# A four-layer image network on one core: layer statistics by ScalarE, buffers lent after layer 1, and the last image's bases by products

## Chip, cores and metric

The program runs on one core of a Trainium2 chip. The metric is the device time of one execution in microseconds (us); for several executions it is the median. The engines are named as in the profile: PE is TensorE (matmuls), DVE is VectorE, ACT is ScalarE, POOL is GpSimd, SP is SyncE, whose queue issues the DMA transfers here.

## What is computed

The input x has 8 images of 32 channels and 256 x 256 places, in fp32. Four layers are applied, each as x + f(group_norm(x)) with 16 groups of two channels:

```
layer 0: 1x1 convolution; its output is also pooled to 5x5 a channel, and that 5x5 is
         the channel's own filter: a 5x5 depthwise convolution of the output
layer 1: q = round(clip(v / 2^-7, -127, 127));  out[o] = -sum over c, 3x3 of |q - w[o]| * 2^-7
layer 2: 3x3 convolution with bias
layer 3: on 8x8 windows, y = layernorm over channels; four functions "kan":
         kan(v) = Ws . exp(-((layernorm(v) - grid_k) / (4/7))^2)  (8 grid points k)
                + Wb . silu(v) + b
         kan1 and kan2 on two 16-wide rearrangements of y, kan3 on y, kan4 on their sum z
```

The group norms need the mean and the variance of whole images, so each layer of an image must be complete before its norm is known.

## The kernel before

**Tiling.** A tile has 128 partitions: 4 row bands of the image times 32 channels. F = 2048 words is 8 rows of 256 places in each band; an image is 8 such chunks (NCH). Between layers the images lie in DRAM (x1, q, x2, x3).

**Stages.** `stage0` is layer 0 in two passes: the first loads 8 chunks, takes statistics (`add_stats`, four `bn_stats` of 512 columns a chunk, L643) and row sums for the pooling (`pool`, L749); the second loads chunks with a halo, does 25 taps of 16 small matmuls on PE (L892), evicts with ACT (L925), takes the statistics of the result, stores it, and at last quantises it (ACT L967, DVE `clip` L972 and L973). `stage1` is layer 1: the 16 passes of an image (4 row parts x 4 output groups) each make 72 distance tiles max(q - w, 0) of 128 x 4128 bf16, by DVE in one instruction (L996) or by ACT in two halves (L998), and PE adds each up with a selection matrix into the accumulator psA (L1018); when a pass is complete ACT evicts psA (L1065, called the gate), statistics are taken of the result, and it is stored. `stage2` is layer 2: load with halo, normalise on DVE (`normal`, L1131), 9 taps on PE (L1148), evict with ACT (L1164), statistics. `stage3` is layer 3, in 8 units an image: centring matmul, eviction (L1234), square (L1239), variance matmul into psV (L1247), 1/sqrt by Ln and Exp (`roots`, L1260 and L1264), broadcast by PE (L1279) and product on DVE (L1287). `kan` then makes 8 bases, each a Square (L1384) and an Exp (L1397) on ACT, and PE sums them into psB (L612), evicted by L1462. Silu runs on ACT (L1328, L1487) with another activation table than Exp and Ln, so each change of table is a load (L1562).

**Order of the work.** Nothing runs in the order in which it is written. Each piece becomes a task with an engine, a cost in us, a rank, its inputs and its buffers; `Plan.run` simulates the four queues while the program is built, always starting the ready task of the lowest rank whose buffers fit, and the instructions are then emitted in that order. Layer 1's distances are no tasks: `fill` makes them where DVE has nothing else ready, on ACT only for the first image or after 8 us without other ACT work (`slack`). PE gives layer 1's sums precedence when two or more distance tiles wait. Layer 1 of image b runs beside layer 3 of image b - 1 and layer 0 of image b + 1 or later. Tasks that need the Exp/Ln table or the Silu table are put into stretches in the order of writing, and a task of a later stretch waits until the earlier ones are all started. A task may have an alternative on another engine (`other`): the square of a basis can be done on DVE as a product (L1390); `run` allows it only when all passes of layer 1 are done.

**Buffers.** `ROOM` gives SBUF to one block of F/2 for psA's results (xr), three blocks for bases (bas), three for silus (si), and an arena of 10 F (sb) for everything else, bases in excess included when BASE_SPARE words stay free. Three distance tiles (dv) exist. In PSUM there are one psA, one psB and two psV. A kan's matmuls may open psB when its exp number HOLD is over.

Of the kernel before, what the change touches and what calls it, by code (L numbers as in the profile page):

```python
# [10 lines left out]
F32 = mybir.dt.float32  # L11
# [13 lines left out]
R = 8  # L25
# [5 lines left out]
DENOM = 4.0 / 7.0  # L31
EPS = 1e-5
# [35 lines left out]
ROOM = [("bas", 3 * BASE, BASE), ("si", 3 * F, F), ("rs", F // 2, F // 4), ("xr", F // 2, F // 2), ("sb", 10 * F, 0)]  # L68
AHEAD = 9.0
# [5 lines left out]
BASE_SPARE = 3 * F  # L75
HOLD = 4
# [14 lines left out]
class Buf:  # L91


    def __init__(self, kind, words=0):
        self.kind, self.words = kind, words
        self.writers, self.readers = [], []
        self.tile = None
        self.left, self.first, self.at, self.taken, self.base = 0, None, None, False, kind == "bas"
        self.spill = False
# [6 lines left out]
class Plan:  # L106
# [57 lines left out]
    def fits(self, need, spare):  # L164
# [3 lines left out]
        for b in need:  # L168
            if b.kind in ("dv", "bas") and b.spill:
                b.kind = "dv" if self.places["dv"] else "bas"  # L170
            if b.base:
                b.kind = "bas" if self.places["bas"] else "sb"
                spare = BASE_SPARE
            if b.kind in self.places and not self.places[b.kind]:
                return False
# [16 lines left out]
    def bases_full(self):  # L192
        return not self.places["bas"] and sum(n for _, n in self.free["sb"]) < F + BASE_SPARE
# [35 lines left out]
    def run(self):  # L229
# [23 lines left out]
        while left or any(not p.done for p in self.passes):  # L253
            moved = True
            while moved:
                moved = False
                for e in engines:
# [3 lines left out]
                    if best is None:  # L261
                        for t in ready[e]:
# [4 lines left out]
                            if t.eng != e and not all(p.done for p in self.passes[self.first_pass :]):  # L267
                                continue
# [4 lines left out]
                        if best is not None and e == "PE" and best.rank > self.image() + AHEAD:  # L273
                            piece = self.fill(e, False)
                            if piece is not None:
                                best = piece
                        if best is not None and best.n is not None:
                            ready[best.eng].remove(best)
                            if best.other:
                                ready[best.other[0]].remove(best)  # L280
                                if best.eng != e:
                                    self.sets[best.stretch][1] -= 1
# [71 lines left out]
    def image(self):  # L354
        return next((p.b for p in self.passes[self.first_pass :] if not p.done), len(self.passes))
# [92 lines left out]
def kernel(  # L448
# [49 lines left out]
    nc.vector.scalar_tensor_tensor(kbsq, kb, -1.0, kb, ALU.mult, ALU.mult)  # L498
    for n in range(5):
# [91 lines left out]
    def sb(b, n=None):  # L591
        return b.tile[:, : n or b.words] if b.tile is not None else arena[:, b.at : b.at + (n or b.words)]
# [25 lines left out]
    class Norm:  # L618
# [17 lines left out]

        def add_stats(self, src, at, r, rank, n=4):
# [8 lines left out]

        def finish(self):
# [5 lines left out]
            def first():  # L653
                for i in range(n):
# [3 lines left out]
            plan.add("DVE", 1.1 if n == 1 else 1.5, first, r=self.bufs, w=[small], rank=self.rank)  # L658
# [70 lines left out]
    def stage0(b, rank, span, after):  # L729
# [9 lines left out]
        for k in range(NCH):  # L739
            xt = Buf("sb", F)  # L740
            plan.add(
                "SP", 2.0, lambda k=k, xt=xt: by_block(lambda p, q: nc.sync.dma_start(sb(xt)[p], xn[k, q])),
# [3 lines left out]
            def pool(k=k, xt=xt):  # L746
                v = sb(xt).rearrange("p (r w) -> p r w", w=W)
# [3 lines left out]
            norm.add_stats(xt, 4 * k, [], r(0.02 * k))  # L751
            plan.add("DVE", 2.9, pool, r=[xt], w=[rs_buf[k]], rank=r(0.02 * k))
# [103 lines left out]
        for k in range(NCH):  # L856
# [60 lines left out]
            for n, t in enumerate(tap_order):  # L917
# [7 lines left out]
                lambda xt=xt: nc.scalar.activation(  # L925
                    sb(xt, F), psB.rearrange("p s f -> p (s f)"), AF.Identity, bias=bi
# [3 lines left out]
            norm1.add_stats(xt, 4 * k, [], rk)  # L930
# [23 lines left out]
        for h in range(NH):  # L954
            for j in range(0, NJ, 2):
# [15 lines left out]
                def clip(t=t):  # L971
                    nc.vector.tensor_scalar(sb(t, F), sb(t, F), QMAX, -QMAX, ALU.min, ALU.max)  # L972
                    nc.vector.tensor_scalar(q16(t), sb(t, F), ROUND, ROUND, ALU.add, ALU.subtract)  # L973

                plan.add("DVE", 2.5, clip, w=[t], rank=rk)
# [51 lines left out]
    def stage1(b, x1buf, qbuf):  # L1027
# [3 lines left out]
        for h in range(NH):  # L1031
# [16 lines left out]
            for g in range(NG):  # L1048
# [3 lines left out]
                ps.xr = xr = Buf("xr", F // 2)  # L1052
# [4 lines left out]
                            sb(xr)[p],  # L1057
# [7 lines left out]
                    lambda g=g, xr=xr: nc.scalar.activation(  # L1065
# [616 lines left out]
```

## Time and profile before

| what | value |
|---|---|
| median of 3 runs | 15807.77 us (15794.59 to 15817.06) |
| profiled execution | 15810.7 us, its span 15808.7 us |
| PE busy | 12814.9 us, 81% |
| DVE busy | 13427.1 us, 85% |
| ACT busy | 12262.5 us, 78% |
| granted PE clock, mean | 0.921 |
| distances on DVE (L996) | 8321 whole, 818 halves |
| distances on ACT (L998) | 972 halves |
| table loads (L1562) | 161 |

The span runs from the first to the last instruction of the profiled execution. Busy is the time in which an engine has an instruction under way. A line such as L996 is a line of the kernel before; a group's row gives its count, its busy time, the mean of one in ns, and the idle time of the engine ahead of it with what ended that. For most of the span three engines are busy at once, so the page's shares are means over stretches in which different engines are the tightest.

### The profile page before, as it was taken

How to read it: one execution, taken by the hardware profiler on the slowest of the kernel's cores; microseconds unless marked ns; L12 is line 12 of the kernel's file. 1: busy time of each engine (PE TensorE's matmuls, PEld its weight loads, DVE VectorE, ACT ScalarE, POOL GpSimd, SP SyncE). 2: the span in 40 equal slices, each digit the busy share in tenths (PEclk: the TensorE clock that was granted, in tenths of full speed). 3: DMA queues.
4: the chain of work that ended last, by engine and by line, in shares of the span. 5: the costliest groups of instructions: out<-in, count | busy, mean ns of one | idle time of the engine just before them, and what ended most of it. 6: DMA issues, size and time to landing. Idle time of an engine off the chain costs nothing.

```text
span 15808.7 us, 560681 instructions
## 1 busy us (share of the span) xinstructions
PE 12814.9 (81%) x260296; PEld 4330.4 (27%) x260296; DVE 13427.1 (85%) x12536; ACT 12262.5 (78%) x6849; POOL 33.1 (0%) x25
## 2 busy tenths in 40 slices
PE   6889897887897888888887888778878887887666
PEld 4223232322222222223222222222222222222222
DVE  2898989789878889888899999999999989997465
ACT  0888848678648778676778997799879987997687
POOL 0000000000000000000000000000000000000000
PEclk9989898998998999999999999999999999998777
DMA  4342345446435444554545554454544454444554
GB/s 117 74 101 55 99 118 160 108 123 169 98 97 157 130 118 125 140 139 105 133 123 142 140 131 126 114 140 123 130 127 130 127 128 129 130 132 112 148 154 134
DMA packets 1192870, 1970.85 MB, mean 125 GB/s; under 512 B 362752, under 2 KB 878848, under 8 KB 1092224
## 3 DMA queue, kind: packets, MB, share of 16 engines
q1 hardware_dynamic: 1190528, 1934.98, 46.6%
q8 instruction: 2036, 33.36, 0.9%
q14 instruction: 306, 2.51, 0.1%
HBM read 1162.83 MB, written 771.75 MB: 122 GB/s over the span
## 4 chain that ended last, share of the span: by engine, by line
PE 22%; ACT 20%; DVE 6%; issue 6%; DMA 1%; SPq 0%; DVEq 0%; ACTq 0%
PE psB L612 9%; PE psA L1018 7%; ACT bas L1384 5%; ACT bas L1397 4%; DVE dv L996 3%; ACT arena L1384 2%; PE psB L1148 2%; ACT arena L1397 2%; ACT arena L1234 2%; PE psB L892 1%; ACT si L1462 1%; ACT arena L1239 1%; DVE arena L1287 1%; PE psV L1247 1%; DVE arena L1390 1%
## 5 line engine op out<-in xcount | busy, mean ns | idle before, releaser
L996 DVE TENSOR_SCALAR dv<-qh,w1q 128x4128 bf16<-128x4128 bf16 (+1 forms) x8815 | 10491.2, 1248 | 1358.8 <-PE psA L1018 1289.9
L1018 PE MATMUL psA<-dv,sel_b 128*32 128x512 bf16 x71048 | 5420.4, 403 | 1421.8 <-DVE dv L996 1155.5
L1018 PEld LDWEIGHTS <-sel_b 128*32 128x32 bf16 x82944 | 2047.6, 97 | 6763.7 <-issue 5758.6
L1384 ACT ACTIVATE bas<-arena,kb 128x2048 f32<-128x2048 f32 x1396 | 2782.5, 1993 | 411.8 <-DVE arena L1287 258.6
L1397 ACT ACTIVATE bas<-bas 128x2048 f32<-128x2048 f32 x1396 | 2671.6, 1914 | 40.1
L998 ACT ACTIVATE dv<-qh,w1n 128x2064 bf16<-128x2064 bf16 x832 | 1635.9, 2009 | 1157.6 <-PE psA L1018 1042.0
L612 PE MATMUL psB<-bas,tl 32*32 32x512 f32 x48544 | 1953.2, 653 | 438.8 <-ACT bas L1397 240.1
L892 PE MATMUL psB<-arena,wt 32*32 32x512 f32 (+1 forms) x51040 | 1848.8, 606 | 122.2 <-issue 69.4
L612 PE MATMUL psB<-arena,tl 32*32 32x512 f32 x22368 | 918.8, 619 | 104.0 <-ACT arena L1397 29.0
L612 PEld LDWEIGHTS psB<-bas,tl 32*32 32x32 f32 x48544 | 526.5, 107 | 1327.5 <-ACT bas L1397 514.2
L892 PEld LDWEIGHTS psB<-arena,wt 32*32 32x32 f32 x51040 | 657.5, 104 | 814.0 <-issue 611.4
L1384 ACT ACTIVATE arena<-arena,kb 128x2048 f32<-128x2048 f32 x407 | 810.0, 1990 | 0.0
L1397 ACT ACTIVATE arena<-arena 128x2048 f32<-128x2048 f32 x407 | 779.1, 1914 | 11.6
L643 DVE BATCH_NORM_STATS2 tiny<-arena 128x6 f32<-128x512 f32 x768 | 473.7, 680 | 345.4 <-ACT arena L925 246.4
L1018 PE MATMUL psA<-qh,sel_b 128*32 128x512 bf16 x9216 | 666.3, 394 | 92.1 <-DMA qh<-q 76.8
L1287 DVE TENSOR_TENSOR arena<-psB,arena 128x2048 f32<-128x2048 f32 x280 | 640.0, 2286 | 59.0 <-PE psB L1279 55.9
L1462 ACT ACTIVATE si<-psB,cols_sb 128x2048 f32<-128x2048 f32 x192 | 377.0, 1963 | 385.0 <-PE psB L612 331.5
L612 PE MATMUL psB<-si,tl 32*32 32x512 f32 x14080 | 618.8, 624 | 32.4 <-DVE arena L1287 13.8
L1148 PE MATMUL psB<-arena,tl 32*32 32x510 f32 (+3 forms) x16384 | 626.6, 610 | 19.9 <-issue 19.8
L1239 ACT ACTIVATE arena<-arena 128x2048 f32<-128x2048 f32 x320 | 612.4, 1914 | 9.8
L925 ACT ACTIVATE arena<-psB,cc 128x2048 f32<-128x2048 f32 x64 | 125.6, 1962 | 536.0 <-PE psB L913 536.0
L1234 ACT ACTIVATE arena<-psB 128x2048 f32<-128x2048 f32 x224 | 418.9, 1870 | 127.1 <-PE psB L612 126.5
(151 smaller groups left out, 7406.4 us busy)
## 6 DMA issues: line engine op xcount, KB each, us to landing
arena<-x SPq DMA_DIRECT2D x128, 1024.0 KB
arena<-y SPq DMA_DIRECT2D x128, 1024.0 KB
si<-sy SPq DMA_DIRECT2D x512, 256.0 KB
arena<-in_x_dram SPq DMA_DIRECT2D x240, 384.0 KB
arena<-in_x_dram SPq DMA_DIRECT2D x256, 256.0 KB
x<-arena SPq DMA_DIRECT2D x256, 256.0 KB
xr<-x SPq DMA_DIRECT2D x512, 128.0 KB
x<-xr SPq DMA_DIRECT2D x512, 128.0 KB
```

The lines of the kernel that those rows point to most:

```text
L612: nc.tensor.matmul(view(o[j * C : (j + 1) * C, i - first, :]), w_, src(rows, i, j), start=start, stop=stop)
L892: nc.tensor.matmul(o[:, lo - 2 * j : hi - 2 * j, c0:c1], wt[rows, t, :], d[rows, lo + dy + 2 : hi + dy + 2, c0 + dx : c1 + dx], start=firs ...
L996: nc.vector.tensor_scalar(dst, src, w1q[:, at : at + 1], 0.0, ALU.subtract, ALU.max)
L998: nc.scalar.activation(dst, src, AF.Relu, bias=w1n[:, at : at + 1])
L1018: nc.tensor.matmul(psA[j * C : (j + 1) * C, i, :], sel_b[:, n, :], src[:, at : at + 2, t % 3 : t % 3 + W], **flags,)
L1148: nc.tensor.matmul(o[:, lo - 2 * j : hi - 2 * j, c0:c1], (wc if t == 4 else tl[:, W2T + t, :])[rows], d[rows, lo + dy + 1 : hi + dy + 1, c ...
L1234: lambda ps=ps, at=at: nc.scalar.activation(sb(c)[:, at], ps().rearrange("p s f -> p (s f)"), func, bias=shift),
L1239: plan.add("ACT", 1.9, lambda: nc.scalar.activation(sb(sq), sb(c), AF.Square), r=[c], w=[sq], rank=rk)
L1287: lambda ps=ps, at=at: nc.vector.tensor_tensor(sb(c)[:, at], ps().rearrange("p s f -> p (s f)"), sb(c)[:, at], ALU.mult),
L1384: lambda k=k, bas=bas: nc.scalar.activation(sb(bas), sb(rb), AF.Square, bias=kb[:, n, k : k + 1]),
L1397: lambda k=k, bas=bas, square=square: nc.scalar.activation(sb(bas), sb(bas), AF.Exp, scale=-1.0, bias=0.0 if square.eng == "ACT" else kbsq ...
L1462: nc.scalar.activation(sb(o), psB.rearrange("p s f -> p (s f)"), AF.Identity, bias=obias)
```

## The change

1. **Statistics.** `add_squares` takes the place of `add_stats`. The sum of a chunk comes out of the eviction that ACT does anyway, through its accumulator output (`accum_out`); for the first pass of layer 0 it comes from the pooling's row sums, less the columns that two bins share. A Square on ACT, shifted by the first chunk's mean, writes its squares as bf16 to spare room behind the chunk and gives their sum through the accumulator output. `first` makes mean and variance of these sums. The blocks grow for it: layer 0's first pass and layer 2 hold 1.5 F each, xr holds 3F/4.
2. **Layer 2's normalisation** moves from DVE to ACT.
3. **The clip** rounds first and clips then, in bf16.
4. **Lent buffers.** When all passes of layer 1 are done (`over`), the distance tiles may be bases or silus. In the same time evictions and squares of `variance` may run on DVE.
5. **The last image's bases.** Two of eight (k = 2 and 5) are made by Square and Exp. The others are products of a neighbour, a constant and one of two ratios, exp(2v) and exp(-2v) times a factor: one DVE instruction each, in the order of CHAIN. The bases' squares have no alternative on DVE there.
6. **The last image's silu** is v * exp(-ln(1 + exp(-v))): a clamp on DVE, three ACT instructions with the Exp/Ln table, a product on DVE.
7. HOLD goes from 4 to 3, BASE_SPARE from 3 F to 2 F, the test with AHEAD goes; the units' order is written anew (`beside`), with each piece given its rank.

The diff, cut:

```diff
+CHAIN = ((2, None), (5, None), (3, 2), (1, 2), (4, 5), (6, 5), (0, 1), (7, 6))
+MID, FAR, FAR2 = 3, 20.0, 50.0
...
-ROOM = [("bas", 3 * BASE, BASE), ("si", 3 * F, F), ("rs", F // 2, F // 4), ("xr", F // 2, F // 2), ("sb", 10 * F, 0)]
-AHEAD = 9.0
+ROOM = [("bas", 3 * BASE, BASE), ("si", 3 * F, F), ("rs", F // 2, F // 4), ("xr", 3 * F // 4, 3 * F // 4), ("sb", 10 * F, 0)]
...
-BASE_SPARE = 3 * F
-HOLD = 4
+BASE_SPARE = 2 * F
+HOLD = 3
...
             if b.base:
-                b.kind = "bas" if self.places["bas"] else "sb"
+                b.kind = "bas" if self.places["bas"] else "dv" if self.over() and self.places["dv"] else "sb"
                 spare = BASE_SPARE
+            if b.side:
+                b.kind = "si" if self.places["si"] or not self.over() else "dv" if self.places["dv"] else "sb"
...
-                        if best is not None and e == "PE" and best.rank > self.image() + AHEAD:
-                            piece = self.fill(e, False)
-                            if piece is not None:
-                                best = piece
...
+    def over(self):
+        return all(p.done for p in self.passes[self.first_pass :])
...
+        def add_squares(self, src, at, i, size, rank):
+            if not self.chunks & 1 << i:
+                self.chunks |= 1 << i
+                plan.add(
+                    "DVE", 0.16,
+                    lambda: nc.vector.tensor_scalar(
+                        self.shift[:, i : i + 1], self.sums[:, at : at + 1], -1.0 / size, None, ALU.mult
+                    ),
+                    r=[src, self.summed], w=[self.shifted[i]], rank=rank,
+                )
+            plan.add(
+                "ACT", 0.25 + 0.85e-3 * size,
+                lambda: nc.scalar.activation(
+                    sb(src)[:, size : size + size // 2].bitcast(BF16), sb(src, size), AF.Square, bias=self.shift[:, i : i + 1],
+                    accum_out=self.squares[:, at : at + 1],
+                ),
+                r=[src, self.shifted[i]], w=[self.bufs[at]], rank=rank,
+            )
...
             def first():
+                if self.chunks:
+                    mean, d, q = self.mv[:, :, 0], self.v, self.t
+                    for of, a in ((d, self.sums), (q, self.squares)):
+                        a = a[:, 0 : 2 * NH * n if n == 1 else NH * n].rearrange("p (n k) -> p n k", n=n)
+                        nc.vector.tensor_reduce(of, a, AX.X, ALU.add)
+                    count = float(HB * W // n)
+                    nc.vector.tensor_scalar(mean, d, 1.0 / count, None, ALU.mult)
+                    nc.vector.tensor_tensor(d, mean, self.shift, ALU.add)
+                    nc.vector.tensor_tensor(d, d, d, ALU.mult)
+                    nc.vector.scalar_tensor_tensor(self.mv[:, :, 1], q, 1.0 / count, d, ALU.mult, ALU.subtract)
+                    return
...
-            xt = Buf("sb", F)
+            xt = Buf("sb", 12 * W)
...
+                total, both = norm.sums[:, k : k + 1], norm.d[:, 0, 0:1]
+                nc.vector.tensor_reduce(total, rowsum[:, :, k * R : (k + 1) * R], AX.XY, ALU.add)
+                nc.vector.tensor_reduce(both, v[:, :, 51:205:51], AX.XY, ALU.add)
+                nc.vector.tensor_tensor(total, total, both, ALU.subtract)
...
-                    sb(xt, F), psB.rearrange("p s f -> p (s f)"), AF.Identity, bias=bi
+                    sb(xt, F), psB.rearrange("p s f -> p (s f)"), AF.Identity, bias=bi,
+                    accum_out=norm1.sums[:, k : k + 1],
...
-            norm1.add_stats(xt, 4 * k, [], rk)
+            norm1.add_squares(xt, k, 0, F, rk)
...
-                    nc.vector.tensor_scalar(sb(t, F), sb(t, F), QMAX, -QMAX, ALU.min, ALU.max)
                     nc.vector.tensor_scalar(q16(t), sb(t, F), ROUND, ROUND, ALU.add, ALU.subtract)
+                    nc.vector.tensor_scalar(q16(t), q16(t), QMAX, -QMAX, ALU.min, ALU.max)
...
-                norm.add_stats(xr, 8 * g + 2 * h, [], rk, 2)
+                norm.add_squares(xr, NH * g + h, g, F // 2, rk)
...
-                nc.vector.tensor_scalar(sb(xt), sb(xt), norm.mean, norm.rs, ALU.subtract, ALU.mult)
-            plan.add("DVE", 1.7, normal, r=[norm.done], w=[xt], rank=rk)
+                nc.scalar.activation(sb(xt, 10 * W), sb(xt, 10 * W), AF.Identity, bias=nmr, scale=norm.rs)
+            plan.add("ACT", 2.4, normal, r=[sm["c2"]], w=[xt], rank=rk)
...
+                evict.other = "DVE", 0.15 + 2.1 * us, lambda ps=ps, at=at: nc.vector.tensor_scalar(
+                    sb(c)[:, at], ps().rearrange("p s f -> p (s f)"), shift, None, ALU.add
+                )
+            square = plan.add("ACT", 1.9, lambda: nc.scalar.activation(sb(sq), sb(c), AF.Square), r=[c], w=[sq], rank=rk)
+            square.other = "DVE", 2.3, lambda: nc.vector.tensor_tensor(sb(sq), sb(c), sb(c), ALU.mult)
...
+        def silu(a, rk):
+            if not last:
+                plan.add("ACT", 1.9, lambda: nc.scalar.activation(sb(a), sb(a), AF.Silu), w=[a], rank=rk, table=SILU)
+                return
+            e = Buf("sb", F)
+            plan.add(
+                "DVE", 1.3, lambda: nc.vector.tensor_scalar(sb(e), sb(a), -FAR2, None, ALU.max),
+                r=[a], w=[e], rank=rk, spare=SPARE,
+            )
+            for func, scale_, bias in ((AF.Exp, -1.0, 0.0), (AF.Ln, 1.0, 1.0), (AF.Exp, -1.0, 0.0)):
+                plan.add(
+                    "ACT", 1.9,
+                    lambda func=func, scale_=scale_, bias=bias: nc.scalar.activation(
+                        sb(e), sb(e), func, scale=scale_, bias=bias
+                    ),
+                    w=[e], rank=rk, table=LN_EXP,
+                )
+            plan.add(
+                "DVE", 2.3, lambda: nc.vector.tensor_tensor(sb(a), sb(a), sb(e), ALU.mult), r=[e], w=[a], rank=rk
+            )
...
+            if last:
+                up, down = Buf("sb", F), Buf("sb", F)
+                plan.add(
+                    "DVE", 1.3,
+                    lambda: nc.vector.tensor_scalar(sb(up), sb(rb), kmax[:, n : n + 1], kmin[:, n : n + 1], ALU.min, ALU.max),
+                    r=[rb], w=[up], rank=rk, spare=SPARE,
+                )
+                for o, sign, bias in ((down, -2.0, kdn[:, n : n + 1]), (up, 2.0, kb2[:, n, MID : MID + 1])):
+                    plan.add(
+                        "ACT", 1.9,
+                        lambda o=o, sign=sign, bias=bias: nc.scalar.activation(
+                            sb(o), sb(up), AF.Exp, scale=sign, bias=bias
+                        ),
+                        r=[up], w=[o], rank=rk, table=LN_EXP, spare=SPARE,
+                    )
+            for k, k0 in chain:
+                bas = bases[k]
+                if k0 is not None:
+                    ratio = up if k > k0 else down
+                    by = float(np.exp(2 * (MID - k0) * (k - k0) - 1))
+                    exps.append(plan.add(
+                        "DVE", 2.4,
+                        lambda bas=bas, k0=k0, ratio=ratio, by=by: nc.vector.scalar_tensor_tensor(
+                            sb(bas), sb(bases[k0]), by, sb(ratio), ALU.mult, ALU.mult
+                        ),
+                        r=[bases[k0], ratio], w=[bas], rank=rk,
+                    ))
+                    continue
...
-                square.other = "DVE", 2.45, product
+                square.other = None if last else ("DVE", 2.45, product)
...
-                        "SP", 2.0 if name == "oa" else 8.0, load2, r=[db], w=[a], rank=rk, after=exps[4:5], spare=F,
+                        "SP", 2.0 if name == "oa" else 8.0, load2, r=[db], w=[a], rank=rk, after=exps[(0 if last else 4) :][:1], spare=F,
```

## The prediction

> **What bounds the kernel now.** I cut the span at the last accumulator eviction of each image's layer 1 (every 16th start of L1065: 1875, 3816, 5700, 7607, 9343, 11057, 12770, 14488) and asked for the busy time of each engine in these stretches; columns are stretch, length, PE, PEld, DVE, ACT, POOL, clock, DMA share, GB/s.
>
> ```profile
> 395.00:1875.00 1480.00, 1247.81 (x26038) 455.61 (x26054) 1309.72 (x1607) 1275.46 (x672) 1.55 (x2) 0.90 0.35 83
> 3816.00:5700.00 1884.00, 1600.80 (x33784) 514.00 (x33799) 1627.51 (x1549) 1321.75 (x732) 6.21 (x2) 0.94 0.48 122
> 11057.00:12770.00 1713.00, 1393.10 (x26888) 448.70 (x26884) 1583.20 (x1344) 1486.11 (x836) 3.90 (x2) 0.94 0.49 128
> 14488.00:15809.00 1321.00, 865.85 (x16244) 311.01 (x16244) 723.34 (x442) 943.40 (x579) 0.00 (x0) 0.75 0.53 144
> ```
>
> So: images 4 to 7 of layer 1 have DVE at 92% and ACT at 87%; images 1 to 3 (which also carry nearly all of layer 0's convolutions) have DVE at 86%, PE 85%, ACT 70%; the last 1321 us, where image 7's layers 2 and 3 are alone, have nobody above 72%. The waits, whole span (who waits for whom, total, times, longest):
>
> ```profile
> DVE dv L996 <- PE psA L1018: 1289.9, 1334, 26.2
> PE psA L1018 <- DVE dv L996: 1155.5, 1989, 8.2
> ACT dv L998 <- PE psA L1018: 1042.0, 309, 18.4
> ```
>
> DVE and PE hand three distance buffers to and fro and each loses about 8%: relief of DVE is worth something, not all of itself. In image 2's stretch DVE waits 223 us on PE and PE 106 us on DVE; in image 6's it is 114 and 190. DVE is the tighter one late, PE early.
>
> Second clock: layer 3 of the image before, on ACT. From the evictions L1462, the layer-3 spans of images 3 to 6 start at 8551, 10128, 11696, 13256: one per 1560 to 1577 us, against 1714 for layer 1. Layer 3 is late (image 2's ends at 8449, 842 us after 7607; image 6's at 14575, 87 after 14488) and catches up. Inside one such span and in the stretch of layer 2 before it:
>
> ```profile
> 11243.00:11581.00 338.00, 290.62 (x6156) 96.21 (x6148) 298.42 (x260) 232.95 (x129) 0.00 (x0) 0.96 0.45 113
> 11696.00:12884.00 1188.00, 967.66 (x18513) 308.60 (x18498) 1103.63 (x912) 1103.96 (x621) 3.90 (x2) 0.94 0.49 129
> ```
>
> ACT is 93% busy in the span and 69% in layer 2.
>
> Prices, from the groups kept apart by shape (count, then busy, mean ns, idle before):
>
> ```profile
> L998 ACT ACTIVATE dv<-qh,w1n 128x2064 bf16<-128x2064 bf16 x832 | 1635.9, 2009 | 1157.6 <-PE psA L1018 1042.0 <-DMA qh<-q 46.1 <-DVE dv L996 32.1
> L643 DVE BATCH_NORM_STATS2 tiny<-arena 128x6 f32<-128x512 f32 x768 | 473.7, 680 | 345.4 <-ACT arena L925 246.4 <-ACT arena L1164 73.1 <-DMA arena<-in_x_dram 21.5
> L1390 DVE SCALAR_TENSOR_TENSOR arena<-arena,kb 128x2048 f32<-128x2048 f32 x124 | 285.5, 2346 | 4.2 <-PE psV L1247 3.3 <-issue 0.9
> L643 DVE BATCH_NORM_STATS2 tiny<-xr 128x6 f32<-128x512 f32 x256 | 163.6, 681 | 24.5 <-ACT xr L1065 22.5 <-DMA si<-od 1.5
> L967 ACT ACTIVATE arena<-arena,cc 128x2048 f32<-128x2048 f32 x64 | 132.8, 2087 | 28.8 <-DMA arena<-x 28.8
> L1131 DVE TENSOR_SCALAR arena<-arena,tiny 128x2560 f32<-128x2560 f32 x64 | 102.8, 1608 | 25.1 <-DMA arena<-x 25.1
> ```
>
> **The Trainium skill.** "ScalarE: Activation LUTs", *What ACT_TABLE_LOAD costs*: one element per cycle at 1.2 GHz for every function, about 93 ns for each pointer operand, 1283 ns a table load. The trace agrees (1914 ns with immediates, 1990 with one pointer, 2087 with two; 1283 for 161 loads), so Exp and Ln here cost 1.91 us. Same page, *Table sets*: cheap functions sit in every set, Ln and Exp share one; hence squares need no load. "VectorE: DVE Perf Modes", *Side-by-side*: fp32 single-source ops run two per cycle, bf16 ones four, two-tensor ops in fp32 one; the trace agrees (L973 1227 ns, L1390 2346 ns). "ScalarE activation tables", *What a function is on this engine*, says the accumulator output sums along the free dim, without a price for writing it out; no run here shows one.
>
> **Part by part.** (1) Statistics. Off DVE: 1024 x 0.68 = 696 us in durations, and 64 normalisations x 1.61 = 103; the clip's second step becomes bf16, 1.22 to about 0.75 (L996 of 2064 bf16 takes 0.75), 64 x 0.47 = 30. On DVE: per layer-0 chunk two small reduces and a subtraction, about 0.54, 64 x 0.54 = 35; 56 shifts x 0.15 = 9; the new closing arithmetic, about 1.0 a norm, is what the aggregates cost (33 us in all). Net -785. On ACT: 192 squares of 2048 x 1.99 = 382, 128 of 1024 x 1.14 = 146 (1.99 less 1024 x 0.833 ns), 64 normalisations of 2560 with two pointers x 2.51 (2.087 plus 512 x 0.833 ns) = 161; and 576 accumulator outputs. Their price lies between 0 and the fixed part of an ACTIVATE (1.99 - 2048 x 0.833 ns = 0.28); below 0 is excluded; I take 0.15: 86 us. Net about +775. ACT's distances give way first: they cost 4.02 for DVE's 1.29, and run only when ACT is idle.
>
> By stretch. Layer-1 images 0 to 3: layer-0 statistics of seven images 7 x 64 x 0.68 = 305, layer 1's 87, layer 2's 65, normalisations 39, clips 26, less 35: -487 on DVE. ACT is at 70 to 86%, a good part of it (899 half distances) optional. I take half, -245, because PE is as tight as DVE there. Images 4 to 7: 87 + 87 + 52 less 7 = -219; PE waits more than DVE, so 0.6 of it, -130. Layer 1 then ends at 14488 - 375 = 14113.
>
> Layer 3 of images 3 to 6: ACT gains 18 + 16 + 20 and about 6 of accumulators = 60 us an image; what falls in layer 2's stretch (some 40) has 105 us of idle to hide in. Without this cover it is 60/0.93 = 65. I take a pitch 30 longer. Image 6's layer 3 ends at 14575 - 245 + 4 x 30 = 14450, so it is now 337 us behind layer 1: what was a DVE stall becomes lateness of layer 3.
>
> New waits. Each norm's first square waits for a shift that DVE makes from the first sum: 56 in all, 0.15 us each behind at most one distance of 1.29; behind it on ACT stand layer 3's exps, so at most 80 us over the run, where ACT is idle mostly: 0. The 128 evictions of psA carry an accumulator: if PE is let go only after it, PE's 107.5 us of waits for L1065 grow by 19; it has other work to take. The closing norm waits for a square instead of two to four statistics: 1.1 to 2 us on ACT's queue against 1.4 to 2.7 on DVE's, the same. At the start the first image's statistics leave DVE (43.6 us busy of the first 60, while DMA moves 169 GB/s): 0 to -10, I take 0. No DMA is added or moved on SP's queue but the two loads of layer 3 gated by an earlier exp.
>
> (2) Lent buffers, evictions and squares by DVE: open once all layer-1 passes are done, so also to those 337 us, in which DVE has no distances. I take a fifth off, -67: 14383. In that time layer 2 of image 7 (which takes 205 us alone) runs beside it; before, it stood alone after 14575 (first layer-3 eviction 14793, against 115 us after the preceding image elsewhere): -100.
>
> (3) Bases and silu of image 7. One unit of layer 3 repeats every 128 us (products of equal place at 15060.7, 15188.5, 15316.6):
>
> ```profile
> 15060.00:15190.00 130.00, 91.11 (x1658) 32.62 (x1644) 83.00 (x43) 107.75 (x68) 0.00 (x0) 0.76 0.58 160
> ```
>
> DVE already makes nearly all squares there (245 of 256 at 2.35), so ACT pays 8 x 1.99 a function, and DVE 8 x 2.35. After: ACT 2 squares, 2 exps, 2 ratios = 2 x 1.99 + 2 x 1.91 + 2 x 1.99 = 11.8; DVE 1.29 + 6 x 2.35 = 15.4. Four functions: ACT 63.7 to 47.1, DVE 75.2 to 61.6. Three silus: ACT 5.7 to 17.2, DVE +3 x (1.29 + 2.29) = 10.7. About three table loads, 3.8, go. ACT: -9; DVE: -3. That alone would be little; the other part is order. Between 15139 and 15182 ACT is nearly empty: the silus need the table, everything with the other table queues behind them, and DVE sits 27.7 us on PE psA L1279. With one table other units' exps may go there. ACT is left with 96 us of 128, PE with 91 at its clock of 0.76, which is the floor. I take 112: 8 x 16 = -128; for the longer last silu +8, and about -10 for evictions that DVE takes: -130 in all.
>
> AHEAD's test (9 images ahead) can never hold; ranks and gates for other images are the same numbers: nothing. HOLD 4 to 3 opens the accumulator one exp earlier, up to 3.9 us a function: it moves PE work, does not add any; 0, between -2 and +2 us a function in PE's wait. The bigger xt blocks (F to 1.5 F) delay layer-0 loads, which run images ahead of need: 0.
>
> **Sum.** The profiled execution took 15810.7 (span 15808.7), the runs' median is 15807.8: alike. 14575 - 245 + 120 - 67 = 14383; from there the 1234 that followed 14575, less 100 and 130 = 1004: 15387, with the 2 around the span 15390. I say 15400 (-2.6%).
>
> **Rivals.** *PE eats the early relief:* layer-0 convolutions and gathers leave PE no room, -245 becomes 0. For: DVE waits longer for PE than PE for DVE in image 2. Against: PE waits for DVE there too. Then 15630. *More:* three quarters of DVE's relief come through (-365), units of 106 us (-180): 14575 - 365 + 80 - 66 + 954 = 15180. *ACT becomes the bound, slower:* nothing hides in layer 2, accumulators cost 0.28, pitch +70, and no early gain: 14575 + 280 + 1234 - 130 = 15960; with my tail it decides from a pitch of +57 on (4 x 57 = 228, which is 15808 - 1004 - 2 - 14575). Against: ACT drops distances first. *Nothing:* the two cancel, and the last units stay at 128 because kan1 to kan2 through memory sets them, not tables.
>
> **Chances.** Forecast (15280 to 15520) 0.50; PE rival (to 15776) 0.24; more 0.13; no change 0.04; slower 0.09. About 0.2% is what a measurement tells from no change. Range 15200 to 15730, leaving out some 2 in 10; faster 0.87.
>
> **To see afterwards.** Right: statistics rows on ACT near 1.99 and 1.14; fewer than 972 half distances; layer 1's last eviction near 14110; image 6's layer 3 a few hundred us behind it; units near 112 us with no table load. Wrong: the last layer-1 eviction not before 14350 (PE rival); layer-3 pitch above 1620 (ACT rival); units still at 128; an accumulator row of 0.28 or more.

## The result, and the profile after

The changed kernel takes 15660.7 us in the median (15658.0 to 15677.2), against 15808.5 for the kernel before, measured beside it. The ratio is 0.991, with an interval from 0.9892 to 0.9927. The change makes the kernel faster by 0.9%, inside the range that was given, but by about a third of what was forecast (15400). The profiled execution took 15677.2 us and its span is 15675.3. It is compared with the one of before (span 15808.7), so the difference to be explained is 133 us.

The head of the page of the changed kernel, with the busy time of each engine:

```profile
span 15675.3 us, 560465 instructions
PE 12755.0 (81%) x260296; PEld 4312.0 (28%) x260296; DVE 13159.8 (84%) x12108; ACT 12322.3 (79%) x7441; POOL 17.6 (0%) x25
```

The prices came out much as they were estimated. These are groups of the changed kernel, kept apart by shape (count, then busy us, mean ns, idle before):

```profile
L1053 ACT ACTIVATE dv<-qh,w1n 128x2064 bf16<-128x2064 bf16 x668 | 1319.0, 2011 | 1068.2 <-PE psA L1073 1028.9 <-DVE dv L1051 29.3 <-DMA qh<-q 7.8
L675 ACT ACTIVATE arena<-arena,tiny 128x2048 bf16<-128x2048 f32 x192 | 383.6, 1998 | 67.4 <-DMA arena<-in_x_dram 41.5 <-DVE tiny L668 23.2
L675 ACT ACTIVATION_READ_ACCUMULATOR arena<-arena,tiny 128x1 f32 x192 | 36.0, 187 | 0.0
L675 ACT ACTIVATE xr<-xr,tiny 128x1024 bf16<-128x1024 f32 x128 | 146.1, 1141 | 6.3 <-DVE tiny L668 4.8
L1188 ACT ACTIVATE arena<-arena,cc,tiny 128x2560 f32<-128x2560 f32 x64 | 159.7, 2511 | 0.0
L1679 ACT ACT_TABLE_LOAD x141 | 180.9, 1283 | 2.4
L1028 DVE TENSOR_SCALAR arena<-arena 128x2048 bf16<-128x2048 bf16 x64 | 44.4, 694 | 2.2
L1489 DVE SCALAR_TENSOR_TENSOR dv<-bas,arena 128x2048 f32<-128x2048 f32 x73 | 164.8, 2287 | 14.0 <-PE psB L623 14.0
L1401 ACT ACTIVATE arena<-arena 128x2048 f32<-128x2048 f32 x72 | 136.4, 1906 | 13.6 <-DVE arena L1395 12.3
```

The squares, the normalisation on ACT, the clip in bf16, the neighbour products and the three steps of the new silu are all there, and 20 table loads are gone (161 to 141). The 320 squares of the statistics brought none: with the last image's bases and silu as before (the second experiment) there are 161 again. Half distances on ACT fell from 972 to 833 (this group and one of 165 on other buffers).

The same stretches as before the change, cut again at the last evictions of layer 1 (columns: stretch, length, PE, PEld, DVE, ACT, POOL, clock, DMA share, GB/s):

```profile
395.00:1661.00 1266.00, 1127.71 (x23418) 388.71 (x23418) 1187.66 (x1413) 1197.09 (x707) 1.61 (x2) 0.93 0.32 74
3457.00:5240.00 1783.00, 1507.84 (x30898) 485.40 (x30897) 1554.79 (x1473) 1396.47 (x854) 2.69 (x2) 0.95 0.49 129
10518.00:12274.00 1756.00, 1421.72 (x27164) 457.80 (x27180) 1538.72 (x1291) 1555.95 (x924) 2.59 (x2) 0.93 0.48 128
13946.00:15675.00 1729.00, 1080.86 (x20964) 422.63 (x20964) 1087.81 (x635) 1067.75 (x645) 0.00 (x0) 0.72 0.52 140
```

Image 0's stretch lost 214 us (1480 to 1266) and image 2's 101 (1884 to 1783), but image 6's is 43 us longer (1713 to 1756), and the end, after the last of layer 1, is 408 us longer (1321 to 1729). Layer 1 ends at 13946 where it ended at 14488: 542 us of gain, of which 133 arrive.

**Where they stay.** Layer 3 starts at 2437 before and at 2032 after (first evictions L1462 and L1575), and from there to the end the images follow one another in it. Between the last eviction of one image and the first of the next lie 100 to 135 us where no chunk of layer 0 falls between them (219 ahead of image 7 in the kernel before), and 300 to 400 where five or six do: before, that is one gap of seven (394 us with six chunks), after, it is four (401, 316, 303 and 297 us with five chunks each). So I cut each trace in two at this start. The kernel before:

```profile
0.00:2437.00 2437.00, 1989.84 (x44104) 790.39 (x44104) 1893.97 (x2462) 1581.38 (x832) 2.72 (x12) 0.91 0.39 95
2437.00:15808.00 13371.00, 10825.06 (x216201) 3540.01 (x216192) 11533.14 (x10075) 10681.09 (x6017) 30.41 (x13) 0.92 0.49 130
```

and the kernel after:

```profile
0.00:2032.00 2032.00, 1660.15 (x36037) 652.93 (x36039) 1582.80 (x2164) 1473.38 (x911) 2.77 (x12) 0.92 0.40 98
2032.00:15675.00 13643.00, 11094.84 (x224266) 3659.02 (x224258) 11576.99 (x9946) 10848.90 (x6531) 14.80 (x13) 0.92 0.49 130
```

Layer 3 starts 405 us earlier and takes 272 us longer (13371 to 13643). On PE the longer time is work: it is busy 270 us more (10825 to 11095), with 8065 more matmuls, and idle for the same time, 2546 against 2548 us. Busy and idle time add up to the stretch on every engine (DVE is busy 44 us more in it and idle 228 more, ACT 168 and 104), so the sum shows what PE did there, not yet that PE held the others up. Most of the matmuls are those of layer 0's convolutions, here of each trace after that start (PE by line: count, busy, mean ns):

```profile
L892 PE MATMUL psB<-arena,wt 32*32 32x510 f32 (+2 forms) x25520 | 930.8, 606 | 46.8 <-issue 32.1 <-DVE arena L1287 10.5 <-ACT arena L1234 2.4
```

```profile
L945 PE MATMUL psB<-arena,wt 32*32 32x510 f32 (+3 forms) x31900 | 1163.7, 607 | 62.7 <-issue 48.7 <-DVE arena L1352 8.7 <-ACT arena L1295 3.9
```

The second group has 6380 matmuls and 233 us more. The whole kernel does 51040 of them, for eight images, so this is exactly one image of layer 0 that was done ahead of the start and is now done behind it. Nothing of PE's total is saved by that. Over the whole span PE is busy 60 us less and idle 73 us less, and these are the 133; the idle time that went lies ahead of the start (447 to 372 us).

### The profile page after: what moved, and what is told of

Read it like the earlier page. It is cut to its first block, busy times and chain, and to the rows that moved or that the text cites. A ratio compares the mean times of both kernels' runs of the same rounds, so it can differ in the third digit from the quotient of the medians.

```text
span 15675.3 us, 560465 instructions
## 1 busy us (share of the span) xinstructions
PE 12755.0 (81%) x260296; PEld 4312.0 (28%) x260296; DVE 13159.8 (84%) x12108; ACT 12322.3 (79%) x7441; POOL 17.6 (0%) x25
## 4 chain that ended last, share of the span: by engine, by line
PE 45%; ACT 30%; DVE 11%; issue 9%; DMA 2%; SPq 1%; DVEq 0%; ACTq 0%
PE psA L1073 16%; PE psB L623 11%; PE psB L945 10%; ACT bas L1497 8%; ACT bas L1510 7%; DVE dv L1051 6%; PE psB L1205 4%; ACT arena L1497 2%; ACT arena L1295 2%; ACT si L1575 2%; DVE arena L1352 2%; ACT arena L1510 2%; ACT arena L1303 1%; PE psA L1062 1%; PE psV L1312 1%
## 5 line engine op out<-in xcount | busy, mean ns | idle before, releaser
L1073 PE MATMUL psA<-dv,sel_b 128*32 128x512 bf16 x70800 | 5364.7, 402 | 1213.3 <-DVE dv L1051 1008.3
L623 PE MATMUL psB<-bas,tl 32*32 32x512 f32 x48992 | 1980.8, 650 | 528.2 <-ACT bas L1510 253.3
L1053 ACT ACTIVATE dv<-qh,w1n 128x2064 bf16<-128x2064 bf16 x668 | 1319.0, 2011 | 1068.2 <-PE psA L1073 1028.9
L623 PEld LDWEIGHTS psB<-bas,tl 32*32 32x32 f32 x48992 | 538.5, 107 | 1423.1 <-issue 536.3
L945 PEld LDWEIGHTS psB<-arena,wt 32*32 32x32 f32 x51040 | 618.3, 104 | 796.8 <-issue 639.9
L1352 DVE TENSOR_TENSOR arena<-psB,arena 128x2048 f32<-128x2048 f32 x280 | 640.6, 2288 | 216.4 <-PE psB L1344 210.4
L623 PE MATMUL psB<-arena,tl 32*32 32x512 f32 x17696 | 696.5, 616 | 138.0 <-ACT si L1575 46.3
L1497 ACT ACTIVATE arena<-arena,kb 128x2048 f32<-128x2048 f32 x353 | 702.7, 1991 | 0.2
L1510 ACT ACTIVATE arena<-arena 128x2048 f32<-128x2048 f32 x353 | 675.7, 1914 | 10.2
L1575 ACT ACTIVATE si<-psB,cols_sb 128x2048 f32<-128x2048 f32 x191 | 374.6, 1961 | 360.2 <-PE psB L623 332.7
L1205 PE MATMUL psB<-arena,tl 32*32 32x512 f32 (+3 forms) x16384 | 629.7, 611 | 32.3 <-issue 32.3
L623 PE MATMUL psB<-si,tl 32*32 32x512 f32 x14048 | 618.6, 621 | 39.3 <-ACT si L1575 17.3
L1303 ACT ACTIVATE arena<-arena 128x2048 f32<-128x2048 f32 x286 | 547.5, 1914 | 9.4 <-DVE arena L1300 0.7
L978 ACT ACTIVATE arena<-psB,cc 128x2048 f32<-128x2048 f32 x64 | 125.6, 1963 | 511.6 <-PE psB L966 511.6
L1344 PE MATMUL psB<-rs,tl 32*32 32x512 f32 x8960 | 353.1, 654 | 212.9 <-DVE arena L1352 107.3
```

Source lines behind the costliest of these rows:

```text
L623: nc.tensor.matmul(view(o[j * C : (j + 1) * C, i - first, :]), w_, src(rows, i, j), start=start, stop=stop)
L945: nc.tensor.matmul(o[:, lo - 2 * j : hi - 2 * j, c0:c1], wt[rows, t, :], d[rows, lo + dy + 2 : hi + dy + 2, c0 + dx : c1 + dx], start=firs ...
L1053: nc.scalar.activation(dst, src, AF.Relu, bias=w1n[:, at : at + 1])
L1073: nc.tensor.matmul(psA[j * C : (j + 1) * C, i, :], sel_b[:, n, :], src[:, at : at + 2, t % 3 : t % 3 + W], **flags,)
L1205: nc.tensor.matmul(o[:, lo - 2 * j : hi - 2 * j, c0:c1], (wc if t == 4 else tl[:, W2T + t, :])[rows], d[rows, lo + dy + 1 : hi + dy + 1, c ...
L1303: square = plan.add("ACT", 1.9, lambda: nc.scalar.activation(sb(sq), sb(c), AF.Square), r=[c], w=[sq], rank=rk)
```

## The experiments

Each run is given with its ratio to the kernel before and that ratio's interval. The theory going in was that DVE's relief is real, and that what holds back the end is the last image's units and an order in which something waits. The time of a unit is taken in image 7, from the last eviction L1575 (before: L1462) of its second unit to that of its seventh, divided by five.

**The statistics undone.** All sums and squares go back to bn_stats on DVE, with layer 2's normalisation and the smaller blocks; the bases, the silu and the lent buffers of the change stay.

```diff
-            xt = Buf("sb", 12 * W)
+            xt = Buf("sb", F)
...
-            norm1.add_squares(xt, k, 0, F, rk)
+            norm1.add_stats(xt, 4 * k, [], rk)
...
-                nc.scalar.activation(sb(xt, 10 * W), sb(xt, 10 * W), AF.Identity, bias=nmr, scale=norm.rs)
+                nc.vector.tensor_scalar(sb(xt, 10 * W), sb(xt, 10 * W), norm.mean, norm.rs, ALU.subtract, ALU.mult)
```

> The changed kernel with its statistics, clip order kept, but sums and squares taken back to DVE (bn_stats), the normalisation of layer 2 back on DVE, and the blocks as small as before; last image, lending, HOLD and BASE_SPARE stay as changed. Theory 'layer 3 is one chain from its first unit to the end': the first layer-3 eviction comes about 400 us later again (2437 against 2032 us), the chain after it is as short as in the kernel before (13363 against 13635), so about 15770 us. Rival 'the squares on ACT cost layer 3 more than DVE's relief brings': 15560 us.

Measured: 15793.0 us, 0.9996 (0.9989 to 1.0003). Without this part nothing is left of the gain. In its trace layer 3 starts at 2449 and the last image's quantisation at 8084 (8380 in the kernel before, 10244 in the changed one): the put-off layer 0 belongs to this part too.

**The last image's bases and silu undone.**

```diff
-            chain = CHAIN if last else [(k, None) for k in range(GRID)]
+            chain = [(k, None) for k in range(GRID)]
...
-                square.other = None if last else ("DVE", 2.45, product)
+                square.other = "DVE", 2.45, product
```

(with the Silu table, and the gate of the two loads of layer 3, as in the kernel before)

> The changed kernel with the last image's bases by Square (or product on DVE) and Exp and its silu by the Silu table, as before; everything else as changed. Theory 'a loop of waits sets the unit of layer 3': the unit stays near 128 us, the time near 15660 us (within 40). Rival 'the new bases saved engine work that counted': 15790 us.

Measured: 15659.0 us, 0.9907 (0.9892 to 0.9921), the time of the changed kernel. A unit of the last image takes 130.0 us, against 131.5 with the new bases and 127.3 before. The new code is neither gain nor loss here, though it takes table loads and ACT time away. Something else must set 130 us.

**No trip through memory.** The last image's two buffers between layer 3's functions aren't sent out and back.

```diff
-            if n == 2:
+            if n == 2 and not last:
```

> The changed kernel in which, for the last image alone, kan3 leaves out the two added terms oa and od (the results of kan1 and kan2), so that the path from one function through DRAM to the next is cut; the output of that image lacks these terms. Theory 'the loop z, variance, kan2, od through DRAM, kan3, z sets the unit': the unit falls from 129 to about 105 us, 15470 us. Rival 'engine work sets it': only 2 of 54 matmul groups of a unit go, 3 us, 15640 us.

Measured: 15640.4 us, 0.9896 (0.9881 to 0.9911), with the unit still at 130. This loop through memory, the nearest to the way from kan1 to kan2 that the prediction's rival of no change had named, is not what holds the units. The other transfers of a unit stay.

**The second function's first statistics on roots of their own**, so that units don't share a buffer there:

```diff
-                kan(1, t, ("B", t), turn(t + 0.5))
+                kan(1, t, ("A" if last else "B", t), turn(t + 0.5))
...
+                if last:
+                    prepare(1, t + 1, ("A", t + 1), turn(t + 0.6), gate if now else [])
```

> The changed kernel in which, for the last image, the variance of the second function (kan(1) in the code) is put with that of the first one of its unit instead of with that of the unit before's last, so that its bases no longer wait for z. Same arithmetic. Theory 'the loop sets the unit': unit about 110 us, 15510 us. Rival 'engine work sets it' or 'psB sets it': 15660 us, or some 20 more since a block is held longer.

Measured: 15631.9 us, 0.9887 (0.9872 to 0.9902), unit 129.7. The 100 us or more that the theory expected are not there. A miss: this loop is not it either.

**Few squares.** Only the first square of each norm and group is made and its sum multiplied; the other squares are left out. This takes some 496 us off ACT. The same is done in the other three norms:

```diff
-            norm1.add_squares(xt, k, 0, F, rk)
+            norm1.few_squares(xt, k, 0, F, rk)
...
```

> The changed kernel with only the first square of each norm (of each of the four groups in layer 1) on ACT; the others are left out and the first one's sum is scaled up, so the variances are estimates and the output only near the reference's. DVE's work is as in the changed kernel. It takes 168 x 2.19 + 96 x 1.33 = 496 us from ACT. Theory 'ACT's new work is what lengthens layer 3': some 250 us come off, 15400 us. Rival 'waits in PE's and psB's order lengthen it, ACT has idle time enough': at most 60 us, 15600 us or more.

Measured: 15626.7 us, 0.989 (0.9873 to 0.9906); its interval overlaps that of the changed kernel. ACT's busy time falls by 415 us (12322 to 11907; it takes 36 more half distances), and that is worth some 34 us of the end. The last image's quantisation starts at 9887, which is 357 us of the 2160 that undoing the statistics brings. So in this order the squares' time on ACT is not the bound, and it is not what put off most of layer 0.

**The broadcast earlier.** What remained was the order of the work. In the changed kernel a function of layer 3 ends its norm with two roots on ACT, a broadcast of the result by 32 matmuls (L1344) and two products on DVE (L1352), and only then can its squares start. This is the chain that ended last, in image 7 of the changed kernel (start us, us, what):

```profile
15091.53 0.70 ACT rs L1325
15092.22 0.02 issue
15092.25 0.64 ACT rs L1329
15092.89 0.04 issue
15092.93 1.11 PE psA L1344 x8
15094.04 0.06 PE psB L623 x4
15094.10 0.79 PE psA L1344 x8
15094.89 4.99 PE psB L623 x93
15099.88 0.02 issue
15099.90 4.50 DVE bas L1489 x2
15104.41 0.04 issue
15104.45 3.40 PE psB L623 x91
15107.85 0.94 PE psA L1344 x16
```

and what ACT does meanwhile, in the timeline (in brackets the idle time before it and who ended it):

```profile
15110.08 2.01 ACT L1497 ACTIVATE bas<-arena,kb 128x2048 f32<-128x2048 f32 x1 [17.20 <-DVE arena L1352]
```

Half of the broadcast goes out at 15093. The other half leaves at 15107.85, and ACT is idle for 17.2 us. In PE's queue 184 matmuls of another function (L623) stand between the two halves. But the chain leaves out what DVE does, which matters as much:

```profile
15091.59 4.49 DVE L1489 SCALAR_TENSOR_TENSOR dv<-bas,arena 128x2048 f32<-128x2048 f32 x2
15096.92 2.29 DVE L1489 SCALAR_TENSOR_TENSOR bas<-bas,arena 128x2048 f32<-128x2048 f32 x1 [0.84 <-PE psB L623]
15099.90 2.29 DVE L1489 SCALAR_TENSOR_TENSOR bas<-dv,arena 128x2048 f32<-128x2048 f32 x1 [0.69 <-PE psB L623]
15102.11 2.28 DVE L1489 SCALAR_TENSOR_TENSOR bas<-bas,arena 128x2048 f32<-128x2048 f32 x1
15104.31 1.22 DVE L1352 TENSOR_TENSOR arena<-psA,arena 128x1024 f32<-128x1024 f32 x1
15108.82 1.23 DVE L1352 TENSOR_TENSOR arena<-psA,arena 128x1024 f32<-128x1024 f32 x1 [3.29 <-PE psA L1344]
```

In the last image both halves go through psA, of which there is one, so the second can't be written before DVE has multiplied the first (L1352). This product comes at 15104.31, 9.4 us after its half was broadcast, since DVE works on neighbour products of the other function (L1489) until then, with two short waits for PE; it ends at 15105.53. From then on PE's queue adds some 2 us. So most of this wait is in DVE's queue. In most units one norm is held up in PE's queue (9 to 11 us until its first half is through, where 2 are enough), one like this in DVE's (9 to 10 us), and one in neither.

The edit moves the rank of the broadcast on PE and of its products on DVE forward, by a fifth of a unit:

```diff
-            scale(n, at, rb, rk - 0.2 * span / (U + 4))
+            scale(n, at, rb, rk - 0.4 * span / (U + 4))
```

> The changed kernel in which the broadcast of 1/sqrt and the product before each function have a rank earlier by 0.4 instead of 0.2 of a unit, for all images, so that on PE they stand ahead of the main matmuls of the function before; nothing else. Theory 'layer 3's unit waits because a function's broadcast stands behind the previous function's main matmuls on PE': 7 us a unit in the last image and some in the others, about 15550 us. Rival 'engine work or a loop through z sets it': 15660 us.

Measured: 15553.9 us, 0.9844 (0.9829 to 0.9858), and the unit is 121.5 us. In the changed kernel, the waits of 780 us of last-image units have this line (who waits for whom, total, times, longest):

```profile
ACT bas L1497 <- DVE arena L1352: 186.0, 18, 17.4
```

and in 730 us of them here:

```profile
ACT bas L1497 <- DVE arena L1352: 75.7, 12, 10.1
```

Layer 1 ends 229 us later than in the changed kernel (14175 against 13946), and yet the run is 107 us shorter. That excludes layer 1's end as what sets the time of these two.

**The same for the last image alone:** 0.4 there, 0.2 elsewhere.

> The same earlier rank, for the last image alone. Theory 'broadcast behind main matmuls': the unit of the last image falls from 130 to about 122 us, 15600 us. Rival: 130 us and 15660 us.

Measured: 15596.2 us, 0.9871 (0.9856 to 0.9885), unit 120.8. About 65 of the 107 us come from the last image. Up to it this run is laid out like the changed kernel. In the run before this one the other images have their broadcasts earlier, and layer 0's chunks lie elsewhere too, so the other 40 us or so can't be put down to the broadcasts alone.

**The earlier broadcast, and the normalisation back on DVE.** On top of the earlier broadcast, 64 instructions of 1.6 us are given back to the engine that the change relieves.

```diff
-                nc.scalar.activation(sb(xt, 10 * W), sb(xt, 10 * W), AF.Identity, bias=nmr, scale=norm.rs)
+                nc.vector.tensor_scalar(sb(xt, 10 * W), sb(xt, 10 * W), norm.mean, norm.rs, ALU.subtract, ALU.mult)
...
```

> The earlier rank for all images, and layer 2's normalisation back on DVE (1.61 us there in place of 2.51 on ACT). Theory 'ACT and layer 3's chain set the end, layer 1 does not': faster than the earlier rank alone by some 60 us, 15490 us. Rival 'DVE's distances are still the bound': slower than it by 64 x 1.61 = 100 us, 15650 us.

Measured: 15497.9 us, 0.9809 (0.9794 to 0.9824): faster than without it (0.9829 to 0.9858), and the best version of all, 163 us under the changed kernel. DVE is busy 74 us longer than without it and ACT 143 us shorter, and the kernel is faster, so DVE's busy time as such is not what ends it, though it is the busiest engine of the page. Whether ACT's relief brings the gain or the new place of layer 0's chunks wasn't separated.

**Nothing lent.** The distances' buffers aren't lent to bases and silus.

```diff
-                b.kind = "bas" if self.places["bas"] else "dv" if self.over() and self.places["dv"] else "sb"
+                b.kind = "bas" if self.places["bas"] else "sb"
...
```

> The changed kernel without the lent buffers: distance tiles are never bases or silus; the rest as changed. Theory 'order on PE, not room, sets layer 3 after layer 1': the time stays at 15660 us within 25. Rival 'the lent blocks open the 570 us after layer 1': 15720 us.

Measured: 15662.2 us, 0.9912 (0.9897 to 0.9927). The lent buffers bring nothing.

**No evictions and no squares of the variance on DVE.** The alternative forms are taken out.

```diff
-                evict.other = "DVE", 0.15 + 2.1 * us, lambda ps=ps, at=at: nc.vector.tensor_scalar(
-                    sb(c)[:, at], ps().rearrange("p s f -> p (s f)"), shift, None, ALU.add
-                )
...
-            square.other = "DVE", 2.3, lambda: nc.vector.tensor_tensor(sb(sq), sb(c), sb(c), ALU.mult)
```

> The changed kernel without the evictions and squares of the variances on DVE after layer 1; the rest as changed. They are 50 evictions and 34 squares. Theory 'a shorter turn of the chain in the last image counts, idle engines do not': up to 40 us slower, 15700 us, since these pieces lie in the chain from one function's sum to the next one's bases. Rival 'no matter': 15660 us.

Measured: 15694.9 us, 0.9937 (0.9922 to 0.9951); its unit is 134.2 us. This part is worth about 33 us, against the run before this one on the same chip (15662.2 us, unit 131.8).

**The earlier broadcast without the new bases and silu.** Both edits from above together.

> The earlier rank of the broadcasts for all images, with the last image's bases and silu as in the kernel before. Theory 'the new bases save engine work, which counts as soon as the order lets it': slower than the earlier rank alone by 35 us or more, 15590 us. Rival 'they bring nothing in either order': 15555 us.

Measured: 15597.6 us, 0.9875 (0.9859 to 0.9892), unit 128.5. With the broadcast early, the new bases and silu are worth 44 us; with the old order they were worth nothing (second experiment).

**The kernel before with the earlier broadcast.**

> The kernel before with nothing but the earlier rank of the broadcasts (0.4 in place of 0.2 of a unit). Theory 'layer 3's chain is the end in the kernel before too': some 60 us faster, 15740 us. Rival 'before, DVE and layer 1 set the end': no change, 15800 us.

Measured: 15759.9 us, 0.9975 (0.9967 to 0.9983). The order alone brings 40 us there, 107 us after the change.

The four cases of order and bases can be laid beside one measurement in the traces: the mean time from the end of the second root to the end of the next 32 matmuls of a broadcast, over image 7's norms without its first two, 24 in all.

| Statistics on ACT, and | broadcast done after | unit | median time |
|---|---|---|---|
| old bases, old order | 7.3 us | 130.0 | 15659.0 |
| new bases, old order (the change) | 11.0 us | 131.5 | 15660.7 |
| old bases, early broadcast | 5.4 us | 128.5 | 15597.6 |
| new bases, early broadcast | 6.0 us | 121.5 | 15553.9 |

In the kernel before it is 6.7 us. So the change itself made the broadcast later by 4 us a norm: 2.5 of them on PE, 1.7 in DVE's queue ahead of the first product. The earlier rank takes off 5 us, 2.8 on PE and 2.3 on DVE. That the later broadcast took what the new bases had saved is the likely reading, but these means alone don't set the unit: in the run without evictions on DVE the broadcast is done after 8.4 us and the unit takes 134.2. Which of the two queues counts for more was not tried.

## Why the prediction was right or wrong

**Right: the prices.** The squares cost 2.00 and 1.14 us (1.99 and 1.14 in the sum), the normalisation 2.51 (2.51), the clip 0.69 (0.75), Ln and Exp 1.91 (1.91), a neighbour product 2.29 (2.35). Writing out an accumulator costs 0.19 us (0.15, between 0 and 0.28): 576 of them took 109 us instead of 86.

**Right in sign only: the early relief.** Layer 1's end moved by 542 us, where 375 were forecast. But a good part of that is work put behind it: image 6's layer 3 ends 570 us after it, where it was 87 before and 337 in the forecast.

**Right: layer 2 of image 7 beside image 6's layer 3.** Image 7's first layer-3 eviction comes 120 us after image 6's last one, against 218 before: −98, where −100 was forecast, and as forecast layer 2 of image 7 (evictions from 14190 to 14530) runs while image 6 is still in layer 3.

**Wrong: the path of layer 3, −245 + 120 − 67.** It gave 14383 for the end of image 6's layer 3; it was 14516, −59 instead of −192. The step that failed is the term for layer 0, put at nothing ("delay layer-0 loads, which run images ahead of need: 0"). It came back in the pitch, the time from one image's first layer-3 eviction to the next one's. Image 3's layer 3 starts at 8008 where it started at 8551, −543, where −245 was forecast; from there to the end of image 6's it takes 6508 us where it took 6024, +484, where +120 − 67 was forecast. Layer 3's early start was bought with delay: 330 us less of PE's work (1990 to 1660) stands ahead of layer 3's start, and an image of layer 0 is done behind it. The chunks show where. Between the layer-3 starts of images 3 and 4 lie nine evictions of layer 0 (L978), between those of 4 and 5 two, where there were none; these pitches are 1935 and 1677 us, where they were 1577 and 1568. In the kernel before, too, a pitch with eight chunks is 1910 us long (from image 2 to image 3). The term "pitch +30" had counted ACT's squares only; few squares showed that these 496 us are worth some 34. What put layer 0 off isn't settled: undoing the statistics brings it back, leaving out most squares does not; the larger blocks of the same part, which are in every run that has layer 0 late, were not tried alone. The "fifth off" for lent buffers and DVE evictions, −67, was 0 for the first and about −33 for the second, and hardly in the place meant: image 6's layer 3 ends at 14518 without these evictions and squares and at 14516 with them, and image 7's takes 1062 us in place of 1031.

**Wrong: units of 112 us, −130.** Image 7's layer-3 evictions span 1031 us, where they spanned 1007: +24. The prediction saw that order counts more than busy time there, but the step that failed is the table as what makes the order: the second experiment brings the table loads back, and its unit takes 130.0 us. One unit, where before 91 us of PE, 83 of DVE and 108 of ACT were busy in 130:

```profile
15025.00:15155.00 130.00, 86.75 (x1608) 31.28 (x1608) 95.56 (x54) 82.83 (x50) 0.00 (x0) 0.75 0.57 155
```

ACT's 108 us became 83 (96 were forecast), DVE's 83 became 96, and the unit stayed as long. With 83, 87 and 96 us of 130, no engine is busy all the time. ACT's longest wait, 186 of 780 us, is for the product behind a norm's broadcast. Broadcast and product stand behind other work in PE's and DVE's queues, and moving both forward in the last image alone takes the unit to 120.8 us. The rival of no change had the units right and the reason wrong (memory).

**The sum of the three:** −59 for image 6's end, −98 for layer 2's place, +24 for the units: −133, which is the measured difference of the two spans.

**The wrong side of the reasoning.** The sum began with how much of DVE's and PE's waits for each other a relief of DVE would return. DVE's relief was in part spent again: its busy time fell by 267 us, not 785, because it took 139 more half distances and the last image's products, evictions and silus. PE's idle time behind the start of layer 3 didn't fall at all. The rival in which PE eats the early relief (15630) was the nearest in time, but by luck: its own sign, a last layer-1 eviction not before 14350, failed (13946), and the units that it kept at 112 us took 131.5. The sign set for ACT as the bound, a pitch above 1620, came up at images 3 and 4 (1935 and 1677), but the squares' time on ACT is not the reason.

## What to carry to other kernels

Before an engine's relief is valued, find the chain that ends the run and write it as its start, plus an engine's busy time after that start, plus its idle time there: an earlier start is only a gain as far as no work was put off behind it. Where no engine is busy all the time, as in the units here, look at what is queued in front of the waiting instruction, and in front of what it waits for, on every engine of the chain; here one number of a rank was worth 107 us, against 148 for the whole change. A saving behind such a place shows only once the place is mended, so try both together before judging either.

## What was not expected of the hardware

An ACTIVATE with an accumulator output is followed by an instruction of its own, ACTIVATION_READ_ACCUMULATOR, of 187 to 194 ns, the same for 1024 and 2048 elements. A product of two SBUF operands in fp32 took 2287 ns with a factor given as an immediate (L1489), and 2346 to 2349 with an addend from a column (L1503); the two differ in their first operation as well. In the end of the run, behind layer 1, the granted clock is 0.72 in the changed kernel against 0.92 over the whole. With the early broadcast, where layer 1 ends 229 us later and this stretch is shorter, the same 224266 matmuls behind layer 3's start took PE 67 us less (11095 to 11028). That the clock is the reason was not tested.
